# Masked attention layer on one core: moving mask sums, reciprocal transposes and the first batch's loads to other places in the order of work

## The chip, the cores and the metric

The kernel runs on one core of a Trainium2 chip. The metric is device time of one execution in microseconds (us). The profile is one profiled execution of the same program. Engines are named as the profile names them: PE (TensorE, matmuls), PEld (its weight loads), DVE (VectorE), ACT (ScalarE), POOL (GpSimd), SP (the queue that issues most transfers).

## The reference

Sixteen batches of x, each 512 channels by 1024 tokens, go through self-attention with 8 heads of 64 and are added back to x. One projection serves as query, key and value. The mask (about half of the tokens are 1) removes keys; a masked query row has all its logits zero, so its softmax is uniform and its context is the mean over all tokens.

```python
q = xt @ Wq.T                                    # (B, T, D), per head dk = 64
scores = scale * einsum('bhqd,bhkd->bhqk', qh, qh)
logits = (scores * cmask + (1.0 - cmask) * NEG) * rmask
attn = softmax(logits)
ctx = einsum('bhqk,bhkd->bhqd', attn, qh)
x = x + transpose(ctx @ Wo.T)
```

## The kernel before

Only active tokens take part in attention: they are gathered into 512 to 544 slots per batch, and masked tokens get one shared row, made from the mean of q. Products that need float32 accuracy are split into float16 high and low parts, with three matmuls for each.

**Order by hand.** `run` writes out the order of TensorE's matmuls; TensorE takes them in just that order. The other engines' instructions are ordered when the program is built, by priority (the order of emission, or 300 places earlier under `high_priority`) and by when their inputs are expected; `behind(ins)` puts the instructions of its block after `ins` on their engine. `once(dma, after)` makes a transfer wait for an instruction, mostly `self.beat`, the last matmul written so far. Each engine, and the SP queue, takes its instructions strictly in the order that comes out.

**Steps.** A batch b has 18 steps, 0 to 17: four head pairs p with four quarters each, and two extra steps. At a pair's quarters 0 and 2 stand its two score products (`scores`, 8 to 16 matmuls, L853, followed by four exponentials on ACT, L877). At quarter 0 of the next pair stands `attend` of the pair before (32 matmuls, L902). The dictionary `plan` says what else TensorE does at the first or second half of a step, `free` what other engines are given at its start. Beside batch b's attention this is the work of the next batch n = b + 1 (transposes `xt`, L595; `query`, L624, with a copy on ACT, L628, and a mask product on DVE, L631; `qsplit`, whose parts are spread to the tile xx by four transfers on SP, L658 to L661; `value`, L687, or L684 in batch 0, with a copy on ACT, L691) and of the one before (`project`, L1027, the output product, added to x by L1033 and scattered by POOL).

**Softmax.** Per batch and half of the heads a shift is made: `peaks` (L738, L741: largest squares, in the tile smcol), `top` (a transpose, L747, and a maximum on DVE, L750), `bottom` (a matmul, L757, read by L760, and a few DVE instructions up to L772). After each pair, `recip_sums` (L940 to L949, the tile rcol) makes reciprocals, and `recip_rows` transposes them (L956), copies them (L961) and sends them through DRAM (rd, L965) back to all partitions (rb, L969). `norm` multiplies the context by them (L1009).

**Facts, slots, sources.** For groups of batches, `permute` and `slots` turn the mask into slot numbers (reads at L277 to L280); `facts_sums` counts the padding and sums a test of the mask (L353 to L366), `facts_end` adds that over partitions by a matmul (L375, read at L377); `sources` (L228, L247 to L250) works out which batch comes at which place, `index` the row numbers (L394, L397).

**Buffers.** TensorE's small products rotate through two PSUM buffers, `pm`. The small products of shift, facts and slots share one place, `spot`, in the bank 5 of the tile that holds scores, and so wait for each other's readers.

**First batch.** Queries, values and index are made in a list called `first` ahead of the steps. `self.between` names work put between the score matmuls of the first score product: `largest` after the second, `told` after the sixth. The row sums of x (tile xm, 512 KB a load through two buffers) are made by ACT (L528) or DVE (L535), `sum_all`, two steps after the load. The output weight's four quarters are loaded by `load` (L187) at steps 3, 6, 9, 12 and split by `wide_high` on ACT (L194) and `wide_rest` on DVE (L197).

## Time and profile before

| what | value |
|---|---|
| median of 3 runs | 958.36 us (957.86 to 960.85) |
| the profiled execution | 957.52 us |
| its span | 955.7 us |
| granted TensorE clock | 0.998 |
| PE idle in the span | 955.7 - 928.0 = 27.7 us |
| HBM read, written | 91.36 MB, 33.91 MB |

Times in the profile are us from the span's start. A line of the timeline gives start, length, engine, source line, operation, output and input tiles with shapes, how many in a row, and in brackets the idle time ahead of it with its releaser. In a list of waits stand the total, how often, and the longest.

### The profile page before, as it was taken

To read this page: it belongs to the slowest core of one execution; us is meant where nothing else is said; L and a number is where in the kernel's file an instruction comes from. 1 tells how busy PE (TensorE), PEld (TensorE's weight loads), DVE (VectorE), ACT (ScalarE), POOL (GpSimd) and SP (SyncE) were. 2 spreads that over 40 slices of the span, in tenths; PEclk is the share of its full clock that TensorE was granted. 3 is DMA by queue.
4 is the path that set the end of the run, shared out by engine and by line. 5 is a ranking of instruction groups with operands and counts; after the bars stand their busy time and mean duration, and the time that the engine had idled before them with its cause. 6 is when DMAs were issued, how large, how long until landed. Compare 5 with 4: busy or idle time off the path is not lost.

```text
span 955.7 us, 22822 instructions
## 1 busy us (share of the span) xinstructions
PE 928.0 (97%) x8113; PEld 580.4 (61%) x8113; DVE 719.3 (75%) x2460; ACT 645.4 (68%) x1669; POOL 306.7 (32%) x311
## 2 busy tenths in 40 slices
PE   7898999999999999999999999999999999999997
PEld 4565656566666666666666666666656666565543
DVE  8888678876877767888677788768776787686563
ACT  4778766666676676776767688656767866655651
POOL 2210022150432514325053340613425044253452
PEclk9999999999999999999999999999999999999999
DMA  5866546665676666666567686744767757555552
GB/s 179 221 199 190 160 157 179 170 196 174 179 210 169 191 189 201 201 188 182 172 191 213 202 249 193 201 135 139 228 181 236 219 157 207 148 167 149 176 175 103
DMA packets 78568, 176.30 MB, mean 184 GB/s; under 512 B 14480, under 2 KB 22416, under 8 KB 78448
## 3 DMA queue, kind: packets, MB, share of 16 engines
q1 hardware_dynamic: 57392, 107.09, 39.8%
q0 software_dynamic: 21056, 67.68, 22.2%
q8 instruction: 66, 1.08, 0.5%
q14 instruction: 54, 0.44, 0.2%
HBM read 91.36 MB, written 33.91 MB: 131 GB/s over the span
## 4 chain that ended last, share of the span: by engine, by line
PE 81%; DVE 9%; DMA 4%; ACT 4%; issue 1%; SPq 1%; POOL 0%; POOLq 0%; DVEq 0%; ACTq 0%
PE pss L902 21%; PE pm L1027 17%; PE pss L853 17%; PE pm L624 16%; PE pss L920 2%; ACT p L877 2%; PE pm L595 2%; DVE xl L554 1%; DMA xm<-x_nat_in 1%; PE pm L687 1%; DMA xx<-hl 1%; PE pss L796 1%; DMA xa<-x_in,idx 1%; PE pss L1027 1%; PE pm L956 1%
## 5 line engine op out<-in xcount | busy, mean ns | idle before, releaser
L877 ACT ACTIVATE p<-pss,nm 128x528 f32<-128x528 f32 (+2 forms) x512 | 354.3, 703 | 98.4 <-PE pss L853 95.4
L902 PE MATMUL pss<-p,v 128*64 128x264 f32 (+2 forms) x2048 | 242.4, 389 | 0.6 <-DVE sc L280 0.6
L853 PE MATMUL pss<-xx 128*128 128x118 f16 (+17 forms) x1856 | 213.8, 287 | 1.4 <-ACT p L877 1.1
L1096 POOL DMA_INDIRECT y_out<-xa,idx x68 | 79.3, 1166 | 411.1 <-DVE nq L762 114.3
L902 PEld LDWEIGHTS pss<-p,v 128*64 128x64 f32 x2048 | 141.3, 137 | 86.5 <-issue 7.1
L853 PEld LDWEIGHTS <-xx 128*128 128x128 f16 (+1 forms) x1856 | 103.8, 96 | 82.3 <-issue 34.9
L624 PE MATMUL pm<-xh,wqh 128*128 128x264 f16 (+5 forms) x512 | 141.8, 277 | 1.5 <-DVE xl L554 0.5
L624 PE MATMUL pm<-xh,wql 128*128 128x264 f16 (+5 forms) x512 | 141.1, 276 | 0.0
L624 PE MATMUL pm<-xl,wqh 128*128 128x264 f16 (+5 forms) x512 | 141.0, 275 | 0.0
L624 PEld LDWEIGHTS <-wqh 128*128 128x128 f16 x1024 | 96.6, 97 | 28.2 <-issue 9.2
L491 POOL DMA_INDIRECT xa<-x_in,idx x68 | 73.6, 1083 | 111.7 <-DMA y_out<-xa,idx 35.8
L877 ACT ACTIVATION_READ_ACCUMULATOR p<-pss,nm 128x1 f32 x512 | 105.5, 206 | 0.0
L1027 PE MATMUL pm<-woh,ch 128*128 128x512 f16 x240 | 91.1, 380 | 0.0
L1027 PE MATMUL pm<-woh,cl 128*128 128x512 f16 x240 | 90.9, 379 | 0.0
L1027 PE MATMUL pm<-wol,ch 128*128 128x512 f16 x240 | 90.9, 379 | 0.0
L628 ACT ACTIVATE q<-pm 128x264 f32<-128x264 f32 (+5 forms) x128 | 50.8, 398 | 43.2 <-PE pm L624 43.0
L1096 POOL DMA_INDIRECT y_out<-xi,idx x60 | 66.0, 1099 | 37.7 <-PE pss L796 17.8
L1033 DVE SCALAR_TENSOR_TENSOR xa<-pm,xa 128x512 f32<-128x512 f32 x61 | 41.7, 684 | 44.2 <-PE pm L1027 44.1
L691 ACT COPY v<-pm 128x512 f32<-128x512 f32 x62 | 36.4, 586 | 56.1 <-PE pm L687 55.8
L1027 PEld LDWEIGHTS <-ch 128*128 128x128 f16 x480 | 44.5, 98 | 47.4 <-issue 4.1
L491 POOL DMA_INDIRECT xi<-x_in,idx x60 | 60.2, 1003 | 21.0 <-issue 16.8
L925 ACT COPY c<-pss 128x528 f32<-128x528 f32 (+2 forms) x64 | 38.2, 598 | 40.5 <-PE pss L920 26.6
(253 smaller groups left out, 1486.7 us busy)
## 6 DMA issues: line engine op xcount, KB each, us to landing
xm<-x_nat_in SPq DMA_DIRECT2D x60, 512.0 KB
xx<-hl SPq DMA_DIRECT2D x208, 136.0 KB
rb<-rd SPq DMA_DIRECT2D x72, 132.0 KB
xx<-hl SPq DMA_DIRECT2D x48, 128.0 KB
pt<-c SPq DMA_DIRECT2D x36, 132.0 KB
pt<-p SPq DMA_DIRECT2D x36, 132.0 KB
rb<-rd SPq DMA_DIRECT2D x32, 136.0 KB
ub<-ud SPq DMA_DIRECT2D x16, 256.0 KB
```

Source lines behind the costliest of these rows:

```text
L491: dma = self.nc.gpsimd.indirect_dma_start(out=tile[:n], out_offset=None, in_=self.x, in_offset=bass.IndirectOffsetOnAxis(ap=idx, axis=0))
L595: self.pe = nc.tensor.transpose(pt[:, c, :], x[:n, c * P:(c + 1) * P], self.ident[:n, :n]).ins
L624: self.beat = nc.tensor.matmul(pq, lhsT=w[:, c, e * P:(e + 1) * P], rhs=xx[:, c, cols], start=(k == 0), stop=(k == 3 * DC - 1)).ins
L628: self.copied = nc.scalar.activation(s["q"][:, e, cols], pq, AF.Copy, scale=1.0 / (SX * SW)).ins
L691: nc.scalar.copy(v, pv)
L853: m = nc.tensor.matmul(flat[:, c0:c1], lhsT=w, rhs=x, start=banks[n] not in banks[:n], stop=banks[n] not in banks[n + 1:])
L877: e = nc.scalar.activation(t, flat[:, at:at + A], AF.Exp, bias=s["nm"][p // 2][:, p % 2 * 2 + k:p % 2 * 2 + k + 1], scale=SCALE, accum_out ...
L902: mm = nc.tensor.matmul(pav[k * DK:(k + 1) * DK, g], lhsT=s["v"][p][:, i, k * DK:(k + 1) * DK], rhs=ps[k, i][:, cols], start=(i == 3), sto ...
L925: self.context_out = nc.scalar.copy(c[:, :A].rearrange("p (g c) -> p g c", g=2), pav).ins
L1027: mm = nc.tensor.matmul(po[:cols.stop - cols.start], lhsT=a[:, e, cols], rhs=w[:, e, :], start=(e == 0 and k == 0), stop=(e == DC - 1 and ...
L1033: return self.nc.vector.scalar_tensor_tensor(x, po, 1.0 / (SX * SW), x, ALU.mult, ALU.add).ins
L1096: dma = self.nc.gpsimd.indirect_dma_start(out=self.out, out_offset=bass.IndirectOffsetOnAxis(ap=idx, axis=0), in_=x, in_offset=None)
```

## The change

Nine moves; what is computed stays the same.

1. In batch 0's index, `facts_sums(0, 2)` is dropped, and `sources(2, B)` after the gathers. Both now stand in `counted`, called within `bottom` of batch 0 right after the shift's sum (L763).
2. `told` stands after the fourth score matmul of the first score product instead of the sixth.
3. ACT's copies of `query(0, 3, 0)` and `value(0, 2)` are put behind the last exponential written so far.
4. In batch 0, `value(0, 3)` and the x transposes of batch 1 move to later places; `post` (the slots) stands before `query(1, 0)`.
5. Quarters 0 and 1 of the output weight are loaded in `first`, once the second split of q is done; quarters 2 and 3 at steps 6 and 7.
6. In batch 0, the last quarter of the row sums of xm is made three steps after its load.
7. `recip_rows` of pair 1 moves from step 10 (11 in batch 0) to step 12, ahead of `query(2, 1)` (in batch 0 of the value product).
8. `recip_rows` of pair 2 moves from the start of step 15 to step 16, behind the scores. The last batch keeps both as they were.
9. For later groups, `facts_sums` moves from step 7 to step 3, and `facts_end` from step 8, behind the shift's matmul and a value product, to step 7, right behind `query(1, 1)`.

```diff
@@ query
-        with self.tc.high_priority(offset=HPO):
+        with self.behind(*self.exp if b == 0 and e == 3 and g == 0 else ()), self.tc.high_priority(offset=HPO):
             self.copied = nc.scalar.activation(s["q"][:, e, cols], pq, AF.Copy, scale=1.0 / (SX * SW)).ins
@@ value
-        with self.tc.high_priority(offset=HPO):
+        with self.behind(*self.exp if b == 0 and e == 2 else ()), self.tc.high_priority(offset=HPO):
             nc.scalar.copy(v, pv)
@@ bottom
-    def bottom(self, b, g):
+    def bottom(self, b, g, counted=None):
...
         s["top"] = nc.vector.tensor_reduce(nm[:, HG:], t, AX.X, ALU.add).ins
+        if counted:
+            counted()
@@ run
                 self.index(1)
-                self.facts_sums(0, 2)
...
-        first += query(0, 1, 1) + value(0, 0) + value(0, 1) + sums0[5:] + query(0, 2, 0) + query(0, 2, 1)[:1] + g1
-        first += [(0, L(self.sources, 2, B))]
+        first += query(0, 1, 1) + value(0, 0) + value(0, 1) + sums0[5:] + [(0, lambda: self.load("o", 0, None, self.last_hl))] + query(0, 2, 0) + query(0, 2, 1)[:1]
+        first += [(0, lambda: self.load("o", 1, None, self.last_hl))] + g1
...
+        def counted():
+            with self.behind(self.st[0]["top"]):
+                self.facts_sums(0, 2)
+                self.sources(2, B)
+
         def told():
             with self.tc.high_priority(offset=HPO):
-                self.bottom(0, 0)
+                self.bottom(0, 0, counted)
...
-        self.between = {1: largest, 5: told}
+        self.between = {1: largest, 3: told}
...
-                turn = [(0.1, L(self.recip_rows, b, 1))]
+                turn = [(0.1, L(self.recip_rows, b, p)) for p in (1, 2)]
...
-                        post = [(0.3, L(self.slots, *g)) for g in new[0]] + [(0, L(self.facts_sums, *g)) for g in new[1]]
+                        post = [(0.3, L(self.slots, *g)) for g in new[0]]
+                        pre += [(0, L(self.facts_sums, *g)) for g in new[1]]
...
-                                (7, 0): third + q(1, 0) + tp(b, 1), (7, 1): q(1, 1) + post + P_(0) + bt(b, 1), (8, 0): tc(0) + v(0) + end + rng[:2],
-                                (10, 0): tv(0) + tail + q(2, 0) + turn, (11, 0): hot + rng[2:] + early,
-                                (12, 0): q(2, 1), (12, 1): index + P_(1) + v(1), (13, 0): take[:3],
-                                (14, 1): rest + pk(n, 0), (16, 0): P_(2) + take[3:], (16, 1): q(3, 0) + tp(n, 0) + q(3, 1),
+                                (7, 0): third + q(1, 0) + tp(b, 1), (7, 1): q(1, 1) + post + end + P_(0) + bt(b, 1), (8, 0): tc(0) + v(0) + rng[:2],
+                                (10, 0): tv(0) + tail + q(2, 0), (11, 0): hot + rng[2:] + early,
+                                (12, 0): turn[:1] + q(2, 1), (12, 1): index + P_(1) + v(1), (13, 0): take[:3],
+                                (14, 1): rest + pk(n, 0), (16, 0): turn[1:] + P_(2) + take[3:], (16, 1): q(3, 0) + tp(n, 0) + q(3, 1),
...
-                                (3, 0): query(0, 3, 1) + [(0.1, L(self.facts_end, 0, 2))] + x[:1] + value(0, 3) + pk(b, 1),
-                                (5, 0): x[1:4], (5, 1): x[4:],
-                                (7, 0): pre + tp(b, 1) + q(0, 0) + bt(b, 1) + q(0, 1), (8, 1): q(1, 0) + post,
-                                (11, 0): hot + q(1, 1) + turn,
-                                (12, 0): tc(0) + v(0) + rng[:2] + q(2, 0), (13, 0): index + q(2, 1),
+                                (3, 0): query(0, 3, 1) + [(0.1, L(self.facts_end, 0, 2))] + x[:1],
+                                (5, 0): value(0, 3) + x[1:2] + pk(b, 1), (5, 1): x[2:4],
+                                (7, 0): x[4:] + pre + tp(b, 1) + q(0, 0) + bt(b, 1) + q(0, 1), (8, 1): post + q(1, 0),
+                                (11, 0): hot + q(1, 1),
+                                (12, 0): turn[:1] + tc(0) + v(0) + rng[:2] + q(2, 0), (13, 0): index + q(2, 1),
...
-                                (16, 0): q(3, 0) + tp(n, 0) + q(3, 1) + take[3:], (16, 1): bt(n, 0),
+                                (16, 0): turn[1:] + q(3, 0) + tp(n, 0) + q(3, 1) + take[3:], (16, 1): bt(n, 0),
...
-                        free.setdefault(3 * c + 3, []).append(lambda c=c: self.load("o", c, None, self.beat))
+                        if c > 1:
+                            free.setdefault(c + 4, []).append(lambda c=c: self.load("o", c, None, self.beat))
...
-                        free.setdefault(at + (2 if b + 2 in self.extra else 4), []).append(L(self.sum_all, x, c, b == 0 and x == 1))
+                        free.setdefault(at + (2 + (b == 0 and c == DC - 1) if b + 2 in self.extra else 4), []).append(L(self.sum_all, x, c, b == 0 and x == 1))
...
-                            if p != 1 or n == B:
+                            if not p or n == B:
                                 free.setdefault(st + 2, []).append(L(self.recip_rows, b, p))
```

## The prediction

> **What bounds the kernel now.** I read the page's busy times and its chain first. TensorE is busy for 928.0 of 955.7 us, and most of the chain is TensorE's own work. The change leaves every matmul in place, so it can only win back TensorE's idle time, 27.7 us, or add to it.

> ```profile
> PE 928.0 (97%) x8113; PEld 580.4 (61%) x8113; DVE 719.3 (75%) x2460; ACT 645.4 (68%) x1669; POOL 306.7 (32%) x311
> ...
> PE 81%; DVE 9%; DMA 4%; ACT 4%; issue 1%; SPq 1%; POOL 0%; POOLq 0%; DVEq 0%; ACTq 0%
> ```

> Next, TensorE's waits, by the line that waited and the line that released it (total us, times, longest):

> ```profile
> PE pss L747 <- DVE smcol L741: 2.6, 1, 2.6
> PE pss L375 <- DVE nm L760: 2.5, 5, 0.5
> PE pm L956 <- ACT q L628: 1.9, 4, 0.5
> PE pm L595 <- DVE xl L554: 1.5, 1, 1.5
> ...
> PE pm L956 <- DVE rcol L949: 1.3, 2, 1.1
> PE pss L853 <- ACT p L877: 1.1, 2, 0.9
> PE pm L684 <- ACT q L628: 1.0, 1, 1.0
> ...
> PE pss L902 <- DVE sc L280: 0.6, 1, 0.6
> ```

> Nearly all of these lines are instructions that the change moves or whose releaser it moves. L375 and L956 recur over the run; the others happen once, in the first batch. The timeline says where, and what the releaser was doing:

> ```profile
> 24.71 0.33 PE L684 MATMUL pss<-ident,q 128*128 128x128 f32 x1 [0.48 <-DVE q L631]
> 31.97 0.39 ACT L628 ACTIVATE q<-pm 128x256 f32<-128x256 f32 x1
> 32.23 0.60 ACT L691 COPY v<-pm 128x512 f32<-128x512 f32 x1
> 33.56 0.93 PE L853 MATMUL pss<-xx 128*128 128x512 f16 x5 [0.90 <-ACT p L877]
> 37.43 0.66 PE L684 MATMUL pm<-ident,q 128*128 128x128 f32 x4 [1.01 <-ACT q L628]
> 42.02 0.66 PE L595 MATMUL pm<-ident,xa 128*128 128x128 f32 x4 [1.51 <-DVE xl L554]
> 73.07 1.06 ACT L528 ACTIVATE xm<-xm 128x1024 f32<-128x1024 f32 x1 [2.62 <-DMA xm<-x_nat_in]
> 77.17 0.30 PE L747 MATMUL pss<-ident,smcol 128*128 128x128 f32 x1 [2.64 <-DVE smcol L741]
> ```

> At 31.97 two copies stand in ScalarE's queue ahead of the fourth exponential, for which scores then wait. At 73.07 ScalarE stands still for a transfer, and everything up to the 2.64 us wait follows from it. Last, the stretches, to see which engine has room:

> ```profile
> 27.50:46.70 19.20, 15.69 (x115) 9.44 (x114) 14.88 (x45) 14.81 (x41) 5.82 (x5) 1.00 0.89 239
> 388.00:445.00 57.00, 56.93 (x534) 36.74 (x532) 46.86 (x175) 40.80 (x106) 18.32 (x18) 1.00 0.64 188
> ```

> (Length; PE, PEld, DVE, ACT, POOL; clock; DMA share; GB/s.) A middle batch is TensorE alone. In the first batch TensorE idles 3.5 us of 19.2 while VectorE, ScalarE and the DMA engines are nearly full: what is gained there can be eaten there.

> **First batch, queries (before 27.5 us).** Mask sums (9 VectorE instructions) and sources of batches 2 to 15 (5) leave VectorE between 20.18 and 24.74, where the index (L397, 21.67), the masks of q (L631) and the splits queue behind them. TensorE waited 0.32 us at 21.95 for that index and 0.48 at 24.71 for that mask. The index can go at about 20.95, the second mask at 23.6 instead of 24.37. I take 0.3 + 0.45 = 0.75; bounds 0 and 0.80.

> **The shift.** Its matmul L757 moves from behind the sixth score matmul to behind the fourth. It stood at 29.35; its input, the maximum at 28.51, was ready at 28.79. Ahead of it TensorE also stood 0.26 us (28.66 to 28.92), until the second half of the split rows landed, which now come about 1 us earlier. So exponentials start some 0.5 us earlier relative to the scores, 1.25 with the step above (28.6 instead of 29.87). TensorE's own gain: 0.2 (0 to 0.26).

> The 14 instructions now run inside the shift, ahead of okm, ok, the product L772, the third pair's split and the range maxima. Independent ones start 0.08 us apart, those on 224 elements 0.3, so 9 x 0.08 + 3 x 0.3 + 2 x 0.13 = 1.9 us. What waits for that split is the SP queue's spread of xx (32.26) and, behind it, the two xm loads (35.95); scores need it only at 53.13. The mask sums' matmul L375 comes at about 33.8 and finds them ready at about 31. If that cover went, the price is at most the 1.9 us, once.

> **Exponentials first.** With copies of q (0.26 from start to start) and v (0.47) put behind all four exponentials, the fourth starts 0.73 us sooner, and all start 1.25 sooner: the 0.90 wait at 33.56 goes (taken 0.9; bounds 0.73 and 0.9). The delayed copies free buffers that TensorE asks for about 0.9 us later: nothing. The transposes of q's last quarter go behind the next scores: 1.57 us of matmuls cover the copy, so the 1.01 goes (taken 1.0; if exponentials hold ScalarE, 0.3). The x transposes, three tiles in a row through two buffers, are spread around attention's 3.67 us; the 1.51 goes unless VectorE is late with xl. VectorE needs 14.88 + 1.9 = 16.8 us in a stretch that shrinks to about 16, but 2.4 of it are range maxima (four L561) that nobody waits for, so I take 1.2; bounds 0 and 1.51. The last x tile, now right ahead of query(0), is read by the second query only, 1.4 us on.

> **Weight loads.** SP issues the first two, behind the first two spreads (8 x 0.65 us), at about 29 instead of 31.61 and 43.14; the other two move from 52.91 and 60.46 to steps at about 41 and 43. Each takes SP 0.35 to 0.53 us. That puts one more 256 KB load into the fullest stretch: at 239 GB/s, 262144 bytes are 1.1 us for whatever queues with it. The first gather needs up to 5.7 us to land: 27.1 + 5.7 = 32.8, its transposes now at 33.9. The 1.1 just fits; I take nothing, bounds 0 and -1.1. [...]

> **Rest of the first batch.** The slots' matmuls go ahead of a query (1.4 us), so attention no longer waits 0.55 at 55.25 for their readers. The row sums of xm's last quarter go one step later, past the value copy. Taken 1.9 of the 2.64: scores (3,1) ended at 73.03, four exponentials and a copy need 3.0 us, the next scores would come at 79.08 - 2.64 = 76.44, so the late sum (1.06) can push exponentials onto the path by 0.7. Bounds 0.5 (the sum still stands ahead of the copy, and only its load comes sooner) and 2.64. The turned reciprocals of the second pair move behind the spread of xx in SP's queue, which takes the wait for rd (2.4 us, 61.82 to 64.26) from in front of three xx issues; value(1) then loses its 0.19. Together 0.55 + 1.9 + 0.2 = 2.65.

> **Recurring.** L375 moves from behind the shift's matmul to behind query(1): it needs the maximum L750 read, and in those five batches that ended 0.34, 0.27, 0.07, 0.07 and -0.01 us before the next product began. So of 5 x 0.49 a few hundredths stay: 2.2 (bounds 1.9 and 2.45). Its 9 instructions move to step 3, 0.7 us each time on a VectorE with a fifth of the batch free. L956 of the second pair moves behind the scores: in four batches it waited 0.48 for a buffer that VectorE (a 1.23 us L385, then L1033) freed late: 1.9. Scores that it stood before have 3.3 us of margin after the last exponential. L956 of the third pair also goes behind the scores: the 1.10 at 129.53 goes (1.0); the scores keep 1.2 us less the 0.3 of the transpose. SP's rd and rb come 1.8 us later per pair; behind them wait xx(3) and pt, not needed for over 10 us. POOL's queue is passed by nothing.

> **Sum.** 0.75 + 0.2 + 3.1 + 2.65 + 2.2 + 1.9 + 1.0 = 11.8, less 1.3 for waits that appear one step on (the nearest rows: 0.52 for ms at 87.10, 0.48 for a q copy, 0.30 for xl): 10.5. The profiled execution took 957.52 us, span 955.7; the median is 958.36, 0.84 above it. So span 945.2, 947.0 for such an execution, 948 as a median.

> **Rivals.** (1) ScalarE, VectorE and DMA are the first batch's bound: the 3.1 shrinks to 0.7, the 1.9 to 0.5, the 0.75 to 0.3; gain 6.2, 952. For: 14.8 of 19.2 us busy on both. Against: the exponentials' chain itself starts 1.25 earlier.
> (2) Gathers land late by the whole 1.1 us and again 1.1 behind the loads at step 6 and 7: 950. [...] For: DMA 0.89 busy. Against: only 1.2 us of TensorE's waits before were for gathers, 0.9 of it at 13.16.
> (3) Nothing gained: the orders on ScalarE and VectorE come out as before, and L375 and L956 wait as long in their new places: 957 to 958. Against: TensorE's order is written out by hand.
> (4) Slower: rb of the second pair lands too late for the product L1009 at step 16, in 15 batches. In a middle batch: transpose 414.52, rb issued by 419.88, L1009 at 425.69, so 5.8 us, less 1.8 later, less 2.6 to 4.5 for landing (rd's own wait, mean and longest): 1.4 to -0.5. Behind it VectorE has 2.5 us idle (before L1033 at 430.80), so it decides once rb lands 2.5 us after the product's turn; each us beyond is paid 15 times: 948 + 15 = 963 for one. Against: the fourth pair's rows have four steps too, and L1009 waited for rb only 0.7 us in the whole run.

> **Chances.** Forecast 0.55 (alone 944 to 951), (1) 0.20, (2) 0.08, (3) 0.08, (4) 0.09. What a measurement can tell from no change is 0.3%, 2.9 us: faster 0.55 + 0.20 + 0.08 = 0.83, same 0.08, slower 0.09. The range for 8 in 10 takes in (1) and (2) and ends below (3)'s middle: 944 to 957.

> **What would show it.** L375 and L956 gone from TensorE's waits; scores (1,1), at 46.74 with the last x tile done, near 42.7 by that count; no wait at L747 above 1 us; four exponentials in a row from about 28.6. Wrong if new waits for xa, xl or xx show up before 50 us, if ScalarE still stands for xm ahead of the value copy, or if L1009 waits for rb.

## The result and the profile after

The changed kernel takes 954.93 us (median; 952.09 to 957.31) against 958.36 us (956.07 to 961.78) for the kernel before, side by side on one chip: a ratio of 0.9956, with a 95% interval of 0.9939 to 0.9973. It is faster, by 3.4 us. The forecast was 948.0, a gain of 10.5.

The profiled execution of after took 957.31 us, the slowest of its kind, and its span of 955.6 is that of before within 0.1. That helps here: it shows what can go wrong. First its busy times:

```profile
PE 930.2 (97%) x8113; PEld 582.9 (61%) x8113; DVE 721.4 (75%) x2460; ACT 644.6 (67%) x1669; POOL 303.9 (32%) x311
```

TensorE idles 955.6 - 930.2 = 25.4 us, 2.3 less than before. But the same 8113 matmuls were busy 2.2 us longer, so some of them ran slower. TensorE's waits after, in the form that the prediction used (line that waited, line that released, total us, times, longest):

```profile
PE pm L208 <- DVE quad L169: 3.9, 1, 3.9
PE pm L958 <- DVE xl L554: 3.3, 1, 3.3
PE pss L595 <- DMA xa<-x_in,idx: 2.3, 2, 1.9
PE pss L747 <- DVE smcol L741: 2.2, 1, 2.2
...
PE pm L624 <- DVE xl L554: 1.3, 3, 0.8
PE pm L624 <- DVE rr L963: 1.1, 1, 1.1
PE pss L268 <- DVE m L750: 0.9, 1, 0.9
...
PE pm L958 <- DVE rcol L951: 0.2, 1, 0.2
```

(The lines behind the shift stand two higher after than before: L956 is now L958, L1009 L1011, L902 L904.) All the recurring waits, L375's 2.5 and L956's 1.9 and 1.3, are gone or down to 0.2. In their place stand single waits of 3.3, 2.2 and 1.1 us, all in the first batch, and two smaller ones behind it: 0.8 of the 1.3 for xl, at 95.46, and L268's 0.9, at 752.80. L208 and xa wait at the very start, for work and transfers that the change doesn't touch; this execution started 1.0 us later there.

Where each kernel stood along the way is read from the starts of attention. First before (the timeline of TensorE, first four pairs and the last):

```profile
42.61 3.67 PE L902 MATMUL pss<-p,v 128*64 128x256 f32 x32
55.25 3.67 PE L902 MATMUL pss<-p,v 128*64 128x256 f32 x32 [0.55 <-DVE sc L280]
67.11 3.67 PE L902 MATMUL pss<-p,v 128*64 128x256 f32 x32
81.74 3.67 PE L902 MATMUL pss<-p,v 128*64 128x256 f32 x32
...
936.64 3.67 PE L902 MATMUL pss<-p,v 128*64 128x256 f32 x32
```

Then after:

```profile
39.36 3.67 PE L904 MATMUL pss<-p,v 128*64 128x256 f32 x32
58.54 3.67 PE L904 MATMUL pss<-p,v 128*64 128x256 f32 x32
71.61 3.67 PE L904 MATMUL pss<-p,v 128*64 128x256 f32 x32
87.07 3.67 PE L904 MATMUL pss<-p,v 128*64 128x256 f32 x32
...
936.40 3.67 PE L904 MATMUL pss<-p,v 128*64 128x256 f32 x32
```

Three stretches show. Up to the first pair, after is 3.25 us ahead, in spite of its late start. By the fourth pair it is 5.33 us behind. From there to the last pair it wins back 5.33 + 0.24 = 5.57 us, in steps of some 0.6 us per batch that has one of the recurring edits, and with one step back of 0.9 at L268. So the recurring part came as forecast (5.1), and the first batch lost what it should have won.

The loss between 40 and 50 us begins with a reduction on VectorE. Here are the SP queue, ScalarE, VectorE and TensorE in the timeline of after (some lines left out):

```profile
37.38 1.23 SPq L543 DMA_DIRECT2D xm<-x_nat_in  x2
43.66 1.08 ACT L553 ACTIVATE xh<-pm 128x512 f16<-128x512 f32 x2
44.26 1.22 DVE L535 TENSOR_REDUCE ms<-xm 128x1 f32<-128x1024 f32 x1 [2.13 <-DMA xm<-x_nat_in]
...
45.61 0.61 DVE L237 TENSOR_TENSOR hl<-c,given 128x256 f16<-128x256 f16 x1
...
46.59 1.28 DVE L554 SCALAR_TENSOR_TENSOR xl<-pm,xh 128x512 f16<-128x512 f32 x2
47.33 0.48 PE L958 MATMUL pm<-ident,rcol 128*128 128x128 f32 x1 [3.27 <-DVE xl L554]
```

The row sum L535 stands at the head of VectorE's queue from 42.13 and waits 2.13 us for a 512 KB load issued at 37.4. Behind it wait 1.2 us of work on the next group's slots (the line of L237 and one on either side) and then the low parts of two x tiles, and on them a `pm` buffer, and on that TensorE, which idles 3.27 us. Before, this sum came behind the low parts of three tiles (after has two by then), and did not wait:

```profile
41.27 1.29 DVE L554 SCALAR_TENSOR_TENSOR xl<-pm,xh 128x512 f16<-128x512 f32 x2
42.48 1.21 DVE L535 TENSOR_REDUCE ms<-xm 128x1 f32<-128x1024 f32 x1
```

The clock did the rest (windows of after: length; PE, PEld, DVE, ACT, POOL; granted clock; DMA share; GB/s):

```profile
47.00:53.50 6.50, 6.17 (x25) 3.04 (x26) 2.33 (x6) 2.95 (x9) 0.00 (x0) 0.51 0.19 71
53.50:60.00 6.50, 6.50 (x67) 4.49 (x67) 5.87 (x31) 4.42 (x12) 0.00 (x0) 1.00 0.30 101
```

The granted clock was 0.50 from 46.60 to 53.43, which is 6.1 us after the wait. In it the matmuls of L624 start 0.23 us apart (51.23, 51.46, 51.69), behind it 0.12 (53.84, 53.96). The same happened from 80.74 to 84.15, with 3.2 us of it behind a wait of 2.25. Its history in the timeline of after:

```profile
66.76 0.28 PE L624 MATMUL pm<-xh,wqh 128*128 128x272 f16 x1 [1.15 <-DVE rr L963]
70.95 1.11 SPq L971 DMA_DIRECT2D rb<-rd  x2
74.62 1.06 ACT L528 ACTIVATE xm<-xm 128x1024 f32<-128x1024 f32 x1
76.13 0.61 ACT L691 COPY v<-pm 128x512 f32<-128x512 f32 x1
78.61 0.69 DVE L1011 TENSOR_TENSOR c<-c,rb 128x512 f32<-128x512 f32 x1 [1.14 <-DMA rb<-rd]
80.92 0.47 PE L747 MATMUL pss<-ident,smcol 128*128 128x128 f32 x1 [2.25 <-DVE smcol L741]
```

The turned reciprocals of the second pair, now ahead of the value product, hold a `pm` buffer for which TensorE waits 1.15 us (L624). Their rb lands at 78.6, so the norm's product L1011 stands 1.14 us at the head of VectorE's queue, ahead of the squares that L747 transposes. ScalarE's row sum of xm (74.62) still stands ahead of the value copy (76.13).

Three waits and two stretches of low clock account for the fourth pair. The forecast had it 6.7 us earlier; without the 1.0 of the late start it is 4.3 later, 11 us worse. The waits are 3.27 + 1.15 + 2.25 = 6.7, of which the forecast had left 0.7 (2.64 - 1.9), and half of 6.1 + 3.2 us of clock is 4.7 by estimate: 6.7 - 0.7 + 4.7 = 10.7.

### The profile page after: what moved, and what is told of

Same layout as the page of the kernel before. It is cut to its first block, busy times and chain, and to the rows that moved or that the text cites. A ratio compares the mean times of both kernels' runs of the same rounds, so it can differ in the third digit from the quotient of the medians.

```text
span 955.6 us, 22818 instructions
## 1 busy us (share of the span) xinstructions
PE 930.2 (97%) x8113; PEld 582.9 (61%) x8113; DVE 721.4 (75%) x2460; ACT 644.6 (67%) x1669; POOL 303.9 (32%) x311
## 4 chain that ended last, share of the span: by engine, by line
PE 79%; DVE 10%; DMA 7%; ACT 2%; issue 1%; SPq 1%; POOL 0%; POOLq 0%; DVEq 0%; ACTq 0%
PE pss L904 20%; PE pm L1029 16%; PE pss L855 16%; PE pm L624 15%; PE pss L922 2%; DMA xx<-hl 2%; DMA rb<-rd 2%; PE pm L595 2%; PE pm L687 1%; DVE xl L554 1%; DMA rd<-rr 1%; PE pss L798 1%; ACT p L879 1%; PE pm L958 1%; DMA xm<-x_nat_in 1%
## 5 line engine op out<-in xcount | busy, mean ns | idle before, releaser
L904 PE MATMUL pss<-p,v 128*64 128x264 f32 (+2 forms) x2048 | 242.4, 389 | 0.0
L904 PEld LDWEIGHTS pss<-p,v 128*64 128x64 f32 x2048 | 141.4, 137 | 85.8 <-issue 5.4
L624 PE MATMUL pm<-xh,wqh 128*128 128x264 f16 (+5 forms) x512 | 142.9, 279 | 2.8 <-DVE rr L963 1.1
L624 PE MATMUL pm<-xl,wqh 128*128 128x264 f16 (+5 forms) x512 | 142.1, 277 | 0.2 <-DVE xl L554 0.2
L624 PE MATMUL pm<-xh,wql 128*128 128x264 f16 (+5 forms) x512 | 142.2, 278 | 0.0
L624 PEld LDWEIGHTS <-wqh 128*128 128x128 f16 x1024 | 99.5, 99 | 26.8 <-issue 7.0
L628 ACT ACTIVATE q<-pm 128x264 f32<-128x264 f32 (+5 forms) x128 | 50.7, 396 | 50.3 <-PE pm L624 48.8
L691 ACT COPY v<-pm 128x512 f32<-128x512 f32 x62 | 36.3, 586 | 59.3 <-PE pm L687 59.3
L716 DVE TENSOR_TENSOR tmp<-pm,par 128x256 f32<-128x256 f32 x26 | 11.0, 424 | 65.2 <-PE pm L713 65.2
```

The source lines that it names most:

```text
L624: self.beat = nc.tensor.matmul(pq, lhsT=w[:, c, e * P:(e + 1) * P], rhs=xx[:, c, cols], start=(k == 0), stop=(k == 3 * DC - 1)).ins
L628: self.copied = nc.scalar.activation(s["q"][:, e, cols], pq, AF.Copy, scale=1.0 / (SX * SW)).ins
L691: nc.scalar.copy(v, pv)
L904: mm = nc.tensor.matmul(pav[k * DK:(k + 1) * DK, g], lhsT=s["v"][p][:, i, k * DK:(k + 1) * DK], rhs=ps[k, i][:, cols], start=(i == 3), sto ...
```

## The experiments

The theory after this reading: the recurring parts pay 5 us, and in the first batch instructions that wait for a transfer stand at the head of in-order queues, ahead of what TensorE needs next. The rivals: the output weight's early loads crowd out the xm loads, the clock alone takes the gain, or the first batch's parts are worth nothing.

**1. The recurring parts alone**, on the kernel before, whose first batch stays as it was:

```diff
+                turn = [(0.1, L(self.recip_rows, b, p)) for p in (1, 2)]
...
+                        pre += [(0, L(self.facts_sums, *g)) for g in new[1]]
...
+                                (7, 1): q(1, 1) + post + end + P_(0) + bt(b, 1), (8, 0): tc(0) + v(0) + rng[:2],
...
+                                (12, 0): turn[:1] + q(2, 1), (12, 1): index + P_(1) + v(1), (13, 0): take[:3],
+                                (14, 1): rest + pk(n, 0), (16, 0): turn[1:] + P_(2) + take[3:], (16, 1): q(3, 0) + tp(n, 0) + q(3, 1),
...
```

> Undoes every part in the first batch and keeps what recurs (mask sums and reciprocal transposes of later batches). Theory: the recurring parts gain 5.1 us as the sum had it (2.2 + 1.9 + 1.0), and the traces of before and after differ by 5.57 us from the fourth attention (81.74 against 87.07 us) to the end, so 953 us, faster than the changed kernel with its 954.9; the first batch's parts then cost about 2 us net. Rival: the recurring parts gain less and the first batch's parts gain the rest; then this kernel takes 956 us or more.

953.27 us against 958.77, a ratio of 0.9935 (0.9915 to 0.9955): 5.5 us, on 5.1 forecast. The first batch's parts, which the changed kernel has on top, cost it about 1.7 us as a median, though the two intervals overlap. The first batch is that of before, with its late wait at L747, and yet in this execution the clock fell, as it did not in the profile of before (timeline of 1, its windows, then the window of before):

```profile
76.97 0.45 PE L747 MATMUL pss<-ident,smcol 128*128 128x128 f32 x1 [2.38 <-DVE smcol L741]
```

```profile
77.00:80.20 3.20, 3.20 (x15) 2.29 (x16) 1.51 (x2) 1.48 (x6) 0.00 (x0) 0.50 0.33 118
80.20:84.00 3.80, 3.80 (x41) 2.57 (x43) 3.54 (x16) 3.31 (x9) 1.83 (x2) 1.00 0.81 235
```

```profile
76.00:80.90 4.90, 3.73 (x41) 2.74 (x42) 3.59 (x13) 4.27 (x13) 1.05 (x1) 1.00 0.52 188
```

**2. VectorE's row sum behind the splits.** The change, but the first of these sums stands behind the last low part:

```diff
-        with self.behind(self.last_hl), self.nc.allow_low_precision(reason="float32"):
+        with self.behind(self.last_hl, *([self.last_xs] if b == 1 and c == 0 else [])), self.nc.allow_low_precision(reason="float32"):
```

> The changed kernel with one more order on VectorE: the first DVE sum of xm (L535 at 44.26) stands behind the split parts of the x transposes (L554) instead of ahead of them. Theory: the 3.27 us wait of L958 at 47.33 was this sum waiting for its load; it falls below 0.5 us, and the halved clock from about 46.8 to 53.5 us (6.7 us at 0.50, so 3.3 us lost) goes with it: up to 6.6 us, 949 to 951 us as a median. Rival: VectorE's load alone (14 instructions more, range maxima, split) makes the split parts late; then more than 1.5 us of the wait stays and the time is 953 us or more.

951.4 us (0.9932; 0.9906 to 0.9959), but L958 still waited 2.4 us. ScalarE shows why:

```profile
42.76 1.06 ACT L528 ACTIVATE xm<-xm 128x1024 f32<-128x1024 f32 x1 [1.96 <-DMA xm<-x_nat_in]
...
43.81 0.57 ACT L927 COPY c<-pss 128x512 f32<-128x512 f32 x1
44.28 1.09 ACT L553 ACTIVATE xh<-pm 128x512 f16<-128x512 f32 x2
```

The other load's sum stands on ScalarE in the same way, 1.96 us, ahead of the copies that make the high parts. So one sum was only a part of the cause: each of the two holds up what stands behind it on its own engine.

**3. The turn of the second pair back at step 11**, on the change:

```diff
-                                (11, 0): hot + q(1, 1),
-                                (12, 0): turn[:1] + tc(0) + v(0) + rng[:2] + q(2, 0), (13, 0): index + q(2, 1),
+                                (11, 0): hot + q(1, 1) + turn[:1],
+                                (12, 0): tc(0) + v(0) + rng[:2] + q(2, 0), (13, 0): index + q(2, 1),
```

> The changed kernel with the first batch's reciprocal transpose of the second pair back at step 11, as before. Theory: rb of that pair landed late (issued at 72.06, used at 78.61, 1.14 us of wait on VectorE), with the squares behind it; that made the 2.25 us wait of L747 at 80.92 and the second stretch of halved clock (80.9 to 84.1, 1.6 us lost), and the transposed copy made the 1.15 us wait at 66.76: 2 to 5 us, 950 to 953 us. Rival: the wait of L747 comes from the row sum on ScalarE that stands ahead of the value copy (74.62 to 75.66); then it stays above 1.2 us, and the time is 954 us or more.

953.22 us (0.9945; 0.9927 to 0.9963). The wait for rr is gone, so it came from the turn's place. L747's is down to 0.4, but a wait of 1.4 for the value copy (L624 on v, L691) is new just ahead of it: ScalarE's row sum stood 1.58 us for its load ahead of that copy. So L747's wait came only in part from the turn. L958 waited 4.0 here.

**4. Both edits.**

> Both orders together. Theory: the two losses are separate, so the gains add: 945 to 948 us, and TensorE's clock stays at 1.00 after the start. Rival: with the first wait gone, xm's loads and the spreads meet later in the same way, and the time is that of the better one alone, 949 us or more.

952.03 us (0.9943; 0.9921 to 0.9964): they don't add up. L958's wait is 1.0, but the one for v has grown to 2.9, behind another sum on ScalarE:

```profile
71.52 1.06 ACT L528 ACTIVATE xm<-xm 128x1024 f32<-128x1024 f32 x1 [3.02 <-DMA xm<-x_nat_in]
...
72.58 0.56 ACT L927 COPY c<-pss 128x512 f32<-128x512 f32 x1
73.04 0.59 ACT L691 COPY v<-pm 128x512 f32<-128x512 f32 x1
```

When TensorE gets earlier, the sums come to the head of their queue before their loads have landed: this one stood there from 68.50.

**5. All row sums behind the copies.** VectorE's as in 2, and those on ScalarE in the first batch behind the last split or value copy:

```diff
@@ sum_half
-        with self.behind(*self.exp):
+        with self.behind(*self.exp, *(self.copies if b == 2 else [])):
@@ the high parts, and value
+                self.copies = [nc.scalar.activation(self.xh[dst], src, AF.Copy, scale=SX).ins]
...
+            self.copies = [nc.scalar.copy(v, pv).ins]
```

> The order of the second experiment, and on ScalarE the row sums of xm in the first batch stand behind the copy of x or of the value written last, instead of ahead of it. In the second experiment L958 still waited 2.4 us: ScalarE's sum stood at 42.76 with 1.96 us of waiting for its load, ahead of the context's copy and both copies of x. Theory: the sums that wait for xm at the head of the two queues are what the first batch loses; then L958 waits under 0.7 us and L747 under 1.0, the clock stays at 1.00 after the start, and the time is 946 to 949 us. Rival: the stretch is bound by the transfers themselves, and the waits move to xl, xx or scores; 951 us or more.

950.01 us (0.9906; 0.989 to 0.9923). L958 waits 1.0; rr 1.7 and L747 1.5 are left, which are the turn's.

**6. The same with the turn at step 11.**

> The same, with the first batch's reciprocal transpose of the second pair back at step 11. Theory: rb's late landing on VectorE is a loss of its own (1.14 us of wait, and 1.15 us at 66.76 for the transposed copy); without both, 1 to 2 us below the run before, 945 to 947 us. Rival: those waits only showed because everything stood late; then the two runs agree within 1 us.

947.75 us against 958.01, 0.9887 (0.9871 to 0.9902): faster than both kernels, and the time that was forecast for the change, though by orders that the change doesn't have. On the chip of experiment 5, the turn's place alone made 2.3 us in the median, though the two intervals overlap a little.

**7. The output weight's loads back** at steps 3, 6, 9 and 12, all else as in the change:

```diff
-        first += query(0, 1, 1) + value(0, 0) + value(0, 1) + sums0[5:] + [(0, lambda: self.load("o", 0, None, self.last_hl))] + query(0, 2, 0) + query(0, 2, 1)[:1]
-        first += [(0, lambda: self.load("o", 1, None, self.last_hl))] + g1
+        first += query(0, 1, 1) + value(0, 0) + value(0, 1) + sums0[5:] + query(0, 2, 0) + query(0, 2, 1)[:1]
+        first += g1
...
-                        if c > 1:
-                            free.setdefault(c + 4, []).append(lambda c=c: self.load("o", c, None, self.beat))
+                        free.setdefault(3 * c + 3, []).append(lambda c=c: self.load("o", c, None, self.beat))
```

> The changed kernel with only the output weight's loads back at steps 3, 6, 9 and 12. Theory: the sums wait because xm lands late, and the two weight loads ahead of it (issued at about 30) and two more at 42 share the transfers with it: about 1.1 us of load each at 239 GB/s, so L958's wait falls from 3.27 by 1 to 2 us and the time to 952 to 954 us. Rival: xm is late by its issue alone (37.4 us, behind the spread of the third pair's rows, which waits for VectorE); then L958 waits 3 us or more and the time stays at 954 to 956 us.

954.73 us (0.995; 0.9932 to 0.9969), as the change. L958 still waited 2.8. The early loads are not the cause, or at most of 0.5 us of the wait.

**8. The wait filled.** 60 matmuls with unused results run ahead of the transpose that waits:

```diff
+    def busy(self, count):
+        for _ in range(count):
+            self.spotted(self.nc.tensor.matmul(self.spot(P), lhsT=self.on16, rhs=self.on16, start=True, stop=True))
...
+                            if b == 0 and p == 0:
+                                free.setdefault(st + 2, []).append(L(self.busy, 60))
```

> The changed kernel with 60 small matmuls (128x128, about 0.055 us each, 3.3 us, results unused) put into the wait ahead of L958, so that TensorE is busy there; what is computed stays the same. Theory: the wait costs twice, once as 3.27 us of idle time and once by the halved clock behind it (0.50 from about 46.8 to 53.5 us, 3.3 us); with TensorE busy the clock stays at 1.00 there, and the time falls by up to 3 us where the changed kernel had that stretch, to 952 to 953 us as a median. Rival: the clock's low stretch has nothing to do with the idle time, or costs nothing because other engines set the pace there; then 954.5 us or more, and the 0.50 stays.

954.01 us (0.9945; 0.9932 to 0.9959). The windows show TensorE kept busy and the clock kept whole:

```profile
44.00:47.00 3.00, 3.00 (x46) 2.78 (x43) 1.24 (x2) 2.08 (x5) 0.00 (x0) 1.00 1.10 224
47.00:54.00 7.00, 6.82 (x72) 5.05 (x70) 4.70 (x17) 3.56 (x11) 0.00 (x0) 1.00 0.45 154
```

So the low clock there follows from the idle time. This execution met 0.50 in two other places, for 3.4 us each: from 16.12, behind a wait of 2.24 for xa, and from 749.99, behind L268's, here 1.72; the clock's mean over the execution was 0.995. The filling takes as long as the wait did (3.51 us, 3.27 in after), so the time that it wins is the clock's: 0.9 us in the median, within the two intervals. The profiled execution of after, with some 3 us lost there, was a bad one; the clock alone doesn't explain where 7 us of forecast went.

**9. The recurring parts and the sums behind the copies**, without the rest of the first batch's parts, beside **10, the kernel of experiment 6 again**:

> The kernel before with the recurring parts alone (as in the first experiment, 953.3) and the row sums of the third batch's means behind the split and value copies, without the first batch's reordering. If the first batch's reordering is worth something once the sums no longer stand in the queues, this stays clearly above the kernel with everything (947.75): with the late wait at L747 (2.4 us in the first experiment) gone it comes to some 951, and the difference of 3 us or so is what the reordered queries, shift and exponentials are worth. If the reordering is worth nothing and the sums were all, it comes to 948 too.

> The kernel of the sixth experiment again, on the chip of the ninth, so that the two can be compared: 947 to 949 if its time is a property of the kernel, with no wait above 1.1 us behind the first attention; up to 951 if the sixth's was luck with the clock.

953.67 us (0.9945; 0.9929 to 0.9962) and 948.35 us (0.9893; 0.9877 to 0.9908). The best kernel repeats, and 5.3 us lie between the two: once the sums stand behind the copies, the first batch's parts are worth something. Moving the sums gains nothing that the times show for the first batch of before (0.9945 against 0.9935 in 1): in the profile it carries the wait past the value copy to the exponentials (ScalarE in 9), probably because the step's delay of edit 6 is missing, which no run tests alone.

```profile
75.77 1.06 ACT L528 ACTIVATE xm<-xm 128x1024 f32<-128x1024 f32 x1 [2.23 <-DMA xm<-x_nat_in]
...
76.82 0.67 ACT L877 ACTIVATE p<-pss,nm 128x512 f32<-128x512 f32 x1
```

The best kernel, waits in 10:

```profile
...
PE pm L315 <- DVE act L217: 1.4, 1, 1.4
PE pss L855 <- ACT p L803: 1.3, 2, 0.8
PE pm L687 <- DMA xx<-hl: 1.2, 1, 1.2
PE pm L958 <- DVE xl L554: 1.0, 1, 1.0
...
PE pm L595 <- DVE xl L554: 0.6, 1, 0.6
...
```

| kernel | us | ratio to before |
|---|---|---|
| recurring parts alone (1) | 953.27 | 0.9935 |
| recurring parts, sums behind copies (9) | 953.67 | 0.9945 |
| the change | 954.93 | 0.9956 |
| the change, sums behind copies (5) | 950.01 | 0.9906 |
| the change, sums behind copies, turn at 11 (6, 10) | 947.75, 948.35 | 0.9887, 0.9893 |

## Why the prediction was wrong, and where it was right

- **Recurring, 5.1: right.** 5.57 from the fourth to the last pair of after; 5.5 as a median in experiment 1. L375 and both L956 waits left the list. The sum had no term for what these parts bring with them: L268 at about 750 waits for the maximum L750 (0.91 in after, up to 1.72 in 8; none in before or in 3).
- **Queries, 0.75: right.** In the profiled executions of 9 and 10, the last x tile's transposes start at 17.46 and 17.74 and the scores at 27.56 and 27.07: 10.10 against 9.33 us, 0.77 less.
- **Shift and the row of exponentials: as described.** Four start in a row, and the copies follow (ScalarE after):

```profile
30.01 0.69 ACT L879 ACTIVATE p<-pss,nm 128x512 f32<-128x512 f32 x1 [0.59 <-DVE nm L760]
...
32.11 0.69 ACT L879 ACTIVATE p<-pss,nm 128x512 f32<-128x512 f32 x1
...
32.77 0.39 ACT L628 ACTIVATE q<-pm 128x256 f32<-128x256 f32 x1
```

  They start at 30.0 instead of 28.6, 1.0 of it from the late start. The 0.90 and 1.01 waits went. TensorE's own 0.2 didn't come: L757 now waits 0.27 for its maximum.
- **The x transposes, 1.2 of 3.1: wrong.** The step was "the 1.51 goes unless VectorE is late with xl". VectorE was late, more by its order and ScalarE's than by its load: with the sums of both moved, and all other work left, L958's wait fell from 3.27 to 1.0 (5). I added up VectorE's work (16.8 us) and never asked which instruction would stand at its head. In after 0.6 (L595) + 3.27 are waited for xl; even in the best kernel it is 0.58 + 0.97 = 1.55, so the term was 0, its lower bound, at best and about -2.3 as made. I had written that the xm loads stand behind the spread of xx in SP's queue, and priced that by the scores alone, not by the sums that wait for those loads.
- **Rest of the first batch, "taken 1.9 of the 2.64": wrong.** The last sum of xm was moved a step, but its place on ScalarE is chosen by when its load is expected, and it stayed ahead of the value copy: L747 waited 2.25 instead of at most 0.7. That wait needs two cures (5 and 6).
- **The turn of the second pair, 0.2: wrong in sign.** I followed SP's queue and found a gain. I didn't follow the `pm` buffer (1.15 at L624) nor rb's landing in the first batch (1.14 at L1011). Its place cost 2.3 us in the median between 5 and 6.
- **The slots, 0.55: right.** The wait at 55.25 is gone.
- **Weight loads, nothing: right** (7). So was the rejection of rival 2 as far as these loads go.
- **Rivals.** Rival 1 had the place: the first batch is bound by ScalarE, VectorE and transfers, on which TensorE's waits of 3.27, 1.15 and 2.25 us end. But it priced that as gains that shrink to 0.7 and 0.5, never as new waits, and so stopped at 952. Rival 4's mechanism, rb late for the norm's product, came five times in after (L1011 waits for rb 7.4 us in all, against 0.7 once before): at 78.61, 718.26, 750.25, 886.69 and 937.73, the longest 2.55 us at 718.26. Outside the first batch TensorE's waits show one of them, the 0.91 at 752.80, where the maximum L750 stands behind the product. So it was not paid in 15 batches.
- **The range** of 944 to 957 holds the result by luck: its upper end stood for gains that shrink, not for waits that are added.
- **The allowance of 1.3** for waits one step on stood against 6.7 us of them in the profiled execution, and nothing was set aside for the clock.

Still open is how often executions of the change meet the low clock: its times spread over 5.2 us (952.09 to 957.31), the best kernel's over 1.0 (6) and 2.8 (10), but only one execution of each run was profiled.

## What to carry to other kernels

Before you price a stall as gone, list what stands at the head of each in-order queue at that time, and ask of each entry which transfer it waits for; if compute moves earlier and the transfer doesn't, a reduction that nobody needs soon becomes the stall (here 2.13 us on VectorE in after, 1.96 on ScalarE in 2). Order such instructions explicitly behind the copies and splits that feed the bounding engine. A buffer or a round trip through DRAM that is moved must be followed to its next user (here waits of 1.15 us for the buffer and 1.14 for rb), in the fullest stretch above all.

## What was unexpected of the hardware

A stall of TensorE of two to three us can cost more than itself: the granted clock fell to 0.50 with idle times of 3.27 and 2.25 us in after (for 6.8 and 3.4 us), of 2.38 us in experiment 1 and of 1.72 us in experiment 8 (for 3.4 us each), but stayed at 1.00 through 2.64 us in before; with the stall filled by matmuls it stayed whole (8).
